# Six row buffers of four history positions in place of twenty, in a gather-and-score kernel

## The chip, the cores and the metric

The kernel runs on one core of one Trainium2 chip. The metric is the device time of the core in microseconds (us), the median of three runs. A core has five engines that run side by side and meet only at semaphores: PE (TensorE, matrix products and transposes), DVE (VectorE), ACT (ScalarE), POOL (GpSimd) and SP (SyncE, which only issues transfers). Here POOL does nothing but issue indirect transfers (gathers): each takes 128 row numbers, one for each partition, and fetches 128 rows of a table in device memory into an SBUF tile.

## What is computed

For each of 50001 items the reference makes two attention vectors from 32 neighbours. Then it scores, for each of 16384 users, the 100 items of a history against a target:

```python
a_sus = _neighbor_attn(E_in, near_full)
a_inf = _neighbor_attn(E_out, near_full)
...
h = jnp.concatenate([E_hist[history], hist_bi], axis=-1)
t = jnp.concatenate([E_tgt[target], tgt_bi], axis=-1)
x = h * t[:, None, :]
z = jax.nn.relu(jnp.einsum('bld,hd->blh', x, W1) + b1)
scores = jnp.einsum('blh,h->bl', z, W2[0])
exp_A = jnp.exp(scores)
mask = (history != target[:, None]) & (history != 0)
exp_A = exp_A * mask
denom = jnp.sum(exp_A, axis=-1) ** BETA
attn = exp_A / denom[:, None]
result = h * attn[..., None]
s = jnp.sum(result)
...
return jax.nn.sigmoid(pred)
```

`h` and `t` have 128 numbers each (64 of the item's own, 2 x 32 of attention). Only the sum of `result` over everything is used, so the kernel needs of each history row its 128 numbers (for the score) and their sum (for the result).

## The kernel before

**Stage 1** (lines 127 to 269) builds two tables in device memory. `table` has a row of 129 floats for each item: the sum, then the 128 numbers of `h`. `ttab` has the 128 numbers of `t`. It gathers 32 neighbours for each item (L160) and is done at about 17,507 us. The change touches nothing in it.

**Stage 2** (lines 271 to 457) goes through the users in 128 chunks of 128 users (one user for each partition), and in each chunk through the 100 positions in 25 groups of four (`LG = 4`, `NG = 25`). That makes 3200 groups, numbered `s`. One pass of the loop at L432 lists the work of several groups at once, and every engine does its own part in exactly this order (the order is written by hand):

- `gather(s)`, POOL: four indirect transfers (L342) fill the row buffer `rows[s % HB]`, tile name `h`, with 4 x 129 floats for each partition. From group `HB` on, the first of the four waits until the buffer's old content is done with: until the transposes of group `s - HB` have signalled (PE, `turned`, L352), and until the DVE copy of its row sums has run (`hsum`, L370). Each gather also waits for the one issued eight before it, whose counter it shares.
- `turn(s)`, PE: four transposes `hT<-ident,h` (L360) into one of three PSUM tiles (`RP = 3`). It waits for the landing of the group, and for `times_target(s - 3)` (`LH = 3`).
- `hidden(s - 3)`: the product with W1, `z_ps<-xT,w1T` (L389) on PE, then bias and relu on ACT, `z<-z_ps` (L393). The product waits for the ACT step three groups before.
- `scored(s - 6)`, PE: the product with W2, `bank<-z,pick` (L400), added up over the 25 groups of a chunk in one PSUM bank (`LS = 6`).
- `sums(s)` and `times_target(s)`, DVE: the copy `hsum<-h` (L370), then `xT<-hT,tT` (L379), the transposed rows times the target. `xT` waits for the signal of the transposes.

Once a chunk POOL gathers the next chunk's target rows (L309, tile `t`), in the pass of group 5; PE turns them in the pass of group 15. Also once a chunk the scores are turned back, exponentiated, masked and summed (L406 to L427).

**The end** (lines 463 to 481) makes one number from all users, then the 16384 answers.

"Shown late" or "signalled late" below means: the profile has an instruction's start on PE, and the engine that waits for its signal starts much later although nothing else is left to wait for. A group's signals can be followed by the start of its `xT` on DVE, because `xT` waits for nothing but the transposes' signal.

Of the kernel before, what the change touches and what calls it, by code (L numbers as in the profile page):

```python
# [44 lines left out]
NG = L // LG  # L45
W = 1 + D
M = 2
HB = 20
RP = 3
LH = 3  # L50
LS = 6
# [6 lines left out]
def kernel(  # L58
# [60 lines left out]
    u_h = ctx.enter_context(tc.tile_pool(name="u_h", bufs=1))  # L119
    rows = [u_h.tile([P, LG, W], F32, name=f"h{i}") for i in range(HB)]  # L120
    hists = {}
# [149 lines left out]
    with (  # L271
# [15 lines left out]
        def writes(one):  # L287
            writers[-1].append(one)
            if len(writers) > RP:
                for other in writers[len(writers) - 1 - RP]:  # L290
                    covered(one, other)
            return one
# [8 lines left out]
        def after(one, other):  # L301
            tc.add_manual_dep(one.ins, other.ins.name, SYNC, reason="waited for once for all that follows")

        def covered(one, other):
            tc.declare_no_dep(one.ins, other.ins, reason="a later wait or one engine's order covers it")
# [32 lines left out]
        def gather(s):  # L338
            c, g = divmod(s, NG)
            for q in range(LG):  # L340
                l = g * LG + q
                got = landed[s, q] = nc.gpsimd.indirect_dma_start(  # L342
                    out=rows[s % HB][:, q, :],
                    out_offset=None,
# [4 lines left out]
                )  # L349
                if s >= HB:  # L350
                    if q == 0:
                        after(got, turned[s - HB, LG - 1])  # L352
                    if q < LG - 1:
                        covered(got, turned.pop((s - HB, q)))

        def turn(s):
            at[s] = next_bank()
            for q in range(LG):
                turned[s, q] = writes(
                    nc.tensor.transpose(at[s][:, q, :], rows[s % HB][:, q, 1:W], ident)  # L360
                )
# [175 lines left out]
```

## Time and profile before

| | us |
|---|---|
| median of three runs (35853.54 to 35863.02) | 35858.32 |
| profiled execution, its time | 35866.87 |
| profiled execution, its span (first to last instruction) | 35865.1 |
| stage 1, to the last neighbour gather | about 17,507 |
| stage 2, first to last gather of history rows | 17507.9 to 35794.6 |
| from the last gather's start to the end of the span | 70.5 |

The profile's page gives each engine's busy time, the costliest groups of instructions with the idle time ahead of them on their engine, and what ended that idle time ("issue": nothing that the profile shows; "remote": a semaphore signal whose sender the profile cannot match). The timeline view has one row for each instruction: start, duration, engine, line, operation, tiles, and in square brackets the idle time before it. The windows view has the busy time and the count of instructions of each engine in a stretch, with the clock granted to PE (1.00 is full speed) and the transfers' rate. Durations on PE are modelled, starts are measured.

The busy shares over the whole span mix two stages that have different limits, so stage 2 has to be read by itself.

### The profile page before, as it was taken

What the parts mean: (1) busy time and instruction counts of PE and PEld (TensorE: products, weight loads), DVE (VectorE), ACT (ScalarE), POOL (GpSimd) and SP (SyncE); (2) the same over time, 40 slices, a digit from 0 to 9 for tenths busy, and PEclk for the clock granted to TensorE, in tenths of its full rate; (3) what the DMA queues carried; (4) which work ended last, traced back from release to release, by engine and by line L of the source; (5) the groups of instructions that cost most, each with busy time, mean ns of one, the idle gap of its engine ahead of it and who ended that gap; (6) DMA issues with size and microseconds to landing.
All of it is one profiled execution on the core that took longest, in us unless ns stands there. A gap on an engine that the chain in (4) does not pass through costs nothing. (4 is left out here: it accounts for less than half of the span.)

```text
span 35865.1 us, 102226 instructions
## 1 busy us (share of the span) xinstructions
PE 10007.5 (28%) x26243; PEld 3227.4 (9%) x26243; DVE 6894.8 (19%) x9965; ACT 2682.2 (7%) x5698; POOL 25707.9 (72%) x25446
## 2 busy tenths in 40 slices
PE   0000000000000000000255555555555555555555
PEld 0000000000000000000011111111111111111111
DVE  2222222222222222222111111111111111111111
ACT  0000000000000000000011111111111111111111
POOL 7777777777777777777766666666666666666666
PEclk9999999999999999999877777777777777777777
DMA  2111111111111111111111111111111111111111
GB/s 46 27 27 27 27 28 29 27 27 27 27 30 27 27 27 27 30 28 25 36 47 47 48 48 47 48 47 48 47 47 47 47 48 47 47 47 48 47 47 44
DMA packets 1027940, 1362.19 MB, mean 38 GB/s; under 512 B 559904, under 2 KB 614432, under 8 KB 1027360
## 3 DMA queue, kind: packets, MB, share of 16 engines
q0 software_dynamic: 814080, 1265.42, 14.7%
q10 hardware_dynamic: 100480, 38.63, 0.6%
q1 hardware_dynamic: 112800, 51.60, 0.6%
q8 instruction: 218, 3.57, 0.0%
q14 instruction: 362, 2.97, 0.0%
HBM read 1315.31 MB, written 51.50 MB: 38 GB/s over the span
## 5 line engine op out<-in xcount | busy, mean ns | idle before, releaser
L342 POOL DMA_INDIRECT h<-table,hidx x12800 | 12109.6, 946 | 6019.4 <-issue 3368.4
L160 POOL DMA_INDIRECT v<-in_egeo_dram,nidx x12512 | 13476.5, 1077 | 4012.6 <-issue 3944.0
L379 DVE TENSOR_TENSOR xT<-hT,tT 128x512 f32<-128x512 f32 x3200 | 2194.9, 690 | 15148.4 <-remote 9884.4
L321 PE MATMUL hT<-ident,t 128*128 128x128 f32 x128 | 46.8, 366 | 17630.5 <-DMA t<-ttab,tidx 17495.1
L389 PE MATMUL z_ps<-xT,w1T 128*128 128x512 f32 x6400 | 4194.4, 743 | 1745.1 <-ACT z L393 1355.8
L360 PE MATMUL hT<-ident,h 128*128 128x128 f32 x12800 | 2514.7, 328 | 5417.8 <-DVE xT L379 3698.5
L400 PE MATMUL bank<-z,pick 128*25 128x512 f32 x6400 | 4009.4, 714 | 0.0
L175 DVE TENSOR_TENSOR prod<-v,own_ps 128x4096 f32<-128x4096 f32 x196 | 864.4, 4410 | 12858.7 <-DMA v<-in_egeo_dram,nidx 12801.8
L393 ACT ACTIVATE z<-z_ps,b_sb 128x512 f32<-128x512 f32 x3200 | 2139.1, 687 | 15632.6 <-remote 8858.8
L360 PEld LDWEIGHTS hT<-ident,h 128*128 128x128 f32 x12800 | 1621.6, 163 | 8577.3 <-DVE xT L379 4769.4
L321 PEld LDWEIGHTS hT<-ident,t 128*128 128x128 f32 x128 | 19.2, 150 | 17772.6 <-issue 17573.6
L192 ACT ACTIVATE ex<-sc,top 128x32 f32<-128x32 f32 x782 | 227.8, 291 | 16704.6 <-DVE top L186 10993.0
L208 DVE TENSOR_TENSOR wv<-v,ex 128x1024 f32<-128x1024 f32 x782 | 1378.4, 1874 | 355.9 <-ACT ex L192 346.8
L389 PEld LDWEIGHTS z_ps<-xT,w1T 128*128 128x128 f32 x6400 | 1175.8, 230 | 1959.9 <-ACT z L393 1527.8
L182 DVE TENSOR_REDUCE sc<-prod 128x128 f32<-128x4096 f32 x196 | 864.5, 4411 | 6.7
L216 DVE TENSOR_REDUCE att<-wv 128x128 f32<-128x4096 f32 x196 | 864.1, 4409 | 6.0
L400 PEld LDWEIGHTS bank<-z,pick 128*25 128x25 f32 x6400 | 435.4, 109 | 3115.6 <-issue 3115.6
L370 DVE COPY hsum<-h 128x4 f32<-128x4 f32 x3200 | 567.8, 177 | 13.4 <-DMA h<-table,hidx 12.9
L415 PE MATMUL hT<-ident,flat 25*128 25x25 f32 x512 | 67.9, 255 | 1041.1 <-ACT flat L406 442.5
L309 POOL DMA_INDIRECT t<-ttab,tidx x128 | 121.1, 946 | 55.0 <-issue 54.4
L415 PEld LDWEIGHTS hT<-ident,flat 25*128 25x128 f32 x512 | 53.4, 176 | 1189.1 <-ACT flat L406 498.2
L192 ACT ACTIVATION_READ_ACCUMULATOR ex<-sc,top 128x1 f32 x782 | 146.1, 187 | 0.0
(53 smaller groups left out, 849.4 us busy)
## 6 DMA issues: line engine op xcount, KB each, us to landing
h<-table,hidx POOLq DMA_INDIRECT x12800
v<-in_egeo_dram,nidx POOLq DMA_INDIRECT x12512
table<-row ACTq DMA_DIRECT2D x22, 1096.5 KB
own<-in_egeo_dram SPq DMA_DIRECT2D x23, 544.0 KB
row<-in_ehist_dram SPq DMA_DIRECT2D x23, 544.0 KB
ttab<-in_etgt_dram ACTq DMA_DIRECT2D x1, 12500.0 KB
ttab<-row SPq DMA_DIRECT2D x22, 544.0 KB
hidx<-in_history_dram SPq DMA_DIRECT2D x32, 200.0 KB
```

The lines of the kernel that those rows point to most:

```text
L160: nc.gpsimd.indirect_dma_start(out=v[:, m, k].rearrange("p t d -> p (t d)"), out_offset=None, in_=egeo, in_offset=bass.IndirectOffsetOnAxi ...
L175: nc.vector.tensor_tensor(prod[:, 0:n].rearrange("p m k t d -> p m k (t d)"), v.rearrange("p m k t d -> p m k (t d)"), own_ps[:, 0:n].to_b ...
L182: nc.vector.tensor_reduce(sc[:, 0:n].rearrange("p m t k -> p m k t"), prod[:, 0:n], AX.X, ALU.add)
L208: nc.vector.tensor_tensor(wv[:, m, t].rearrange("p d k -> p k d"), subs[b]["v"][:, m, :, t, :], ex[:, m, t, :].rearrange("p (k o) -> p k o ...
L216: nc.vector.tensor_reduce(att[:, 0:n], wv[:, 0:n], AX.X, ALU.add)
L342: got = landed[s, q] = nc.gpsimd.indirect_dma_start(out=rows[s % HB][:, q, :], out_offset=None, in_=table, in_offset=bass.IndirectOffsetOn ...
L360: nc.tensor.transpose(at[s][:, q, :], rows[s % HB][:, q, 1:W], ident)
L370: copy = nc.vector.tensor_copy(users[c]["hsum"][:, g * LG : (g + 1) * LG], rows[s % HB][:, :, 0:1].rearrange("p q o -> p (q o)"),)
L379: times[s] = nc.vector.tensor_tensor(xT[s % XB], at.pop(s), users[c]["tT"].to_broadcast([D, LG, P]), ALU.mult)
L389: first[s] = nc.tensor.matmul(z_ps[s % RP], w1T, xT[s % XB], start=True, stop=True)
L393: second[s] = nc.scalar.activation(z[s % ZB], z_ps[s % RP], AF.Relu, bias=b1_sb)
L400: third[s] = nc.tensor.matmul(bank[c % 2], pick[:, g, :], z[s % ZB], start=g == 0, stop=g == NG - 1)
```

## The change

```diff
-HB = 20
+HB = 6
```

`HB` is the number of row buffers. It is used in `rows` (L120), in `gather` (L343, L350 to L354), and in `turn` and `sums`, which look up the buffer. A buffer holds 4 x 129 x 4 = 2064 bytes for each partition, so the pool shrinks from 41,280 to 12,384 bytes. The product of the scores runs on PE in both kernels (`scored`, L400, is the same in both); no instruction is added, removed or moved.

What differs is a wait. The rows are POOL's own list of instructions, around groups 5 and 6 of the first chunk; `h_102` is the sixth row buffer, `h_103` the seventh, `h_97` the first, and in square brackets stand the counters that an instruction waits for. Before:

```order
12540 L342 DMA h_102<-table,hidx 128x129 [waits DMASW1_49]
12541 L342 DMA h_103<-table,hidx 128x129 [waits DMASW2_49]
12542 L342 DMA h_103<-table,hidx 128x129 [waits DMASW3_49]
12543 L342 DMA h_103<-table,hidx 128x129 [waits DMASW4_49]
12544 L342 DMA h_103<-table,hidx 128x129 [waits DMASW5_49]
12545 L342 DMA h_104<-table,hidx 128x129 [waits DMASW6_49]
```

And now:

```order
12540 L342 DMA h_102<-table,hidx 128x129 [waits DMASW1_49]
12541 L342 DMA h_97<-table,hidx 128x129 [waits DMASW2_49,DVE_49,PE_49]
12542 L342 DMA h_97<-table,hidx 128x129 [waits DMASW3_49]
12543 L342 DMA h_97<-table,hidx 128x129 [waits DMASW4_49]
12544 L342 DMA h_97<-table,hidx 128x129 [waits DMASW5_49]
12545 L342 DMA h_98<-table,hidx 128x129 [waits DMASW6_49,DVE_49,PE_49]
```

Group 6 writes the first buffer again and so waits for DVE and PE. Before, the first group with such a wait was group 20. From group 20 on the lists have the same waits at the same places; the signal that is waited for is that of the group six before in place of twenty before.

## The prediction

> **What bounds the kernel now.** I read the page's groups first, because stage 1 and stage 2 share nothing but POOL:
>
> ```profile
> span 35865.1 us, 102226 instructions
> L342 POOL DMA_INDIRECT h<-table,hidx x12800 | 12109.6, 946 | 6019.4 <-issue 3368.4 <-remote 2070.2 <-DMA h<-table,hidx 265.3
> ```
>
> In stage 2 POOL is busy for 12.1 ms and idle for 6.0 ms. The 3368.4 us of "issue" over 10,991 times are 0.3 us between one gather and the next, part of its pace. The 2070.2 us of "remote" are something else, so I went to the windows and then to the timeline of one piece:
>
> ```profile
> 17507.00:35795.00 18288.00, 9953.97 (x26078) 3209.49 (x26078) 2675.07 (x7508) 2255.17 (x3686) 12229.91 (x12928) 0.72 0.19 47
> 17720.00:26000.00 8280.00, 4549.62 (x11852) 1467.41 (x11850) 1215.62 (x3409) 1026.75 (x1676) 5538.13 (x5856) 0.73 0.19 47
> 26000.00:35790.00 9790.00, 5330.40 (x14068) 1717.61 (x14068) 1442.01 (x4050) 1216.95 (x1990) 6547.72 (x6923) 0.72 0.19 47
> ```
>
> ```profile
> 26455.99 0.94 POOL L342 DMA_INDIRECT h<-table,hidx  x1 [5.54 <-remote]
> 26459.74 0.95 POOL L342 DMA_INDIRECT h<-table,hidx  x1 [0.31 <-issue]
> ...
> 26499.76 0.95 POOL L342 DMA_INDIRECT h<-table,hidx  x1 [0.30 <-issue]
> 26506.86 0.95 POOL L342 DMA_INDIRECT h<-table,hidx  x1 [6.16 <-remote]
> ```
>
> POOL runs in bursts. From 26455.99 to 26459.74 stand three steps of 1.25 us, so a group takes 5.0 us; to 26499.76 it issues 36 transfers (43.77 / 1.25 + 1), nine groups; then it stands 6.16 us. At 1.25 us the stage's 12,928 issues would take 16,160 us of the window's 18,288, so 2,128 us are such pauses. The pace with pauses is very even: 5856 issues in 8280 us and 6923 in 9790 us are both 1.414 us each, and this burst has 50.87 / 36 = 1.413.
>
> What POOL waits for is on DVE, whose `xT` starts when PE's transposes have signalled. Same piece:
>
> ```profile
> 26455.76 0.69 DVE L379 TENSOR_TENSOR xT<-hT,tT 128x512 f32<-128x512 f32 x1 [14.63 <-remote]
> ...
> 26457.77 0.68 DVE L379 TENSOR_TENSOR xT<-hT,tT 128x512 f32<-128x512 f32 x1
> ...
> 26463.90 0.69 DVE L379 TENSOR_TENSOR xT<-hT,tT 128x512 f32<-128x512 f32 x1 [1.65 <-PE hT L360]
> ...
> 26466.70 0.69 DVE L379 TENSOR_TENSOR xT<-hT,tT 128x512 f32<-128x512 f32 x1 [2.03 <-PE hT L360]
> ...
> 26475.81 0.69 DVE L379 TENSOR_TENSOR xT<-hT,tT 128x512 f32<-128x512 f32 x1 [8.34 <-issue]
> ...
> 26495.41 0.69 DVE L379 TENSOR_TENSOR xT<-hT,tT 128x512 f32<-128x512 f32 x1 [18.83 <-remote]
> ...
> 26506.63 0.69 DVE L379 TENSOR_TENSOR xT<-hT,tT 128x512 f32<-128x512 f32 x1 [10.42 <-remote]
> ```
>
> ```profile
> 26465.62 0.66 PE L360 MATMUL hT<-ident,h 128*128 128x128 f32 x4
> 26468.04 0.66 PE L360 MATMUL hT<-ident,h 128*128 128x128 f32 x4
> 26470.46 0.66 PE L360 MATMUL hT<-ident,h 128*128 128x128 f32 x4
> 26496.15 1.11 PE L360 MATMUL hT<-ident,h 128*128 128x128 f32 x4 [12.99 <-issue]
> 26502.44 2.08 PE L389 MATMUL z_ps<-xT,w1T 128*128 128x512 f32 x2 [5.18 <-ACT z L393]
> 26504.45 1.90 PE L400 MATMUL bank<-z,pick 128*25 128x512 f32 x2
> ```
>
> Call the first `xT` that of group n (those of n+1, n+2 and n+4 are left out). Groups n to n+3 come in 2 us (signals that were pending), n+5 and n+6 follow one another by 2.8 us, then n+7 comes after 9.1 us, n+8 after 19.6 us and n+9 after 11.2 us, when POOL has been still for a while. The transposes of n+6, n+7 and n+8 start on PE at 26465.62, 26468.04 and 26470.46; `xT` follows 1.1 us later for n+6 and 24.9 us later for n+8. So while transfers stream, PE's signals come later and later, and a pause of POOL lets them out at once. The profile doesn't say why. Whatever it is, it limits the average, since the pauses come out at the same share everywhere. The bound of stage 2 is this pair: streaming delays PE's signals, late signals fill the row buffers, and full buffers stop the streaming.
>
> **The change, part by part.** No instruction is added or removed, so PE, DVE and ACT have the same work; the score product is on PE before and after. One wait moves: group s on POOL waits for transposes s-6 in place of s-20. Behind it on POOL stand the rest of the gathers and, once a chunk, the target gather, which is issued ten groups (57 us) before PE turns it: no one waits for that. What the wait costs has three terms.
>
> (1) *The steady part.* After a pause, POOL starts group n+20 now, because transposes n have signalled, and may start n+20+j once n+j have. With six buffers it starts n+6 at the same signal and may start n+6+j under the same condition on n+j. At 0.23 + 5.0 j us after the signal its schedule is the same, the next pause comes at the same j (j = 9: due 45.2 us after the signal, transposes n+9 signal at 50.9), and it ends the same way. What can differ is that PE now waits for a landing. The landing is read at the start of the stage, where nothing is ahead:
>
> ```profile
> 17512.10 0.95 POOL L342 DMA_INDIRECT h<-table,hidx  x1 [0.30 <-issue]
> 17514.60 0.20 DVE L370 COPY hsum<-h 128x4 f32<-128x4 f32 x1 [3.63 <-DMA h<-table,hidx]
> ```
>
> 2.50 us from the fourth issue to the first reader. Groups n to n+5 have landed before the signal. Group n+6 is issued from 26455.99, its fourth transfer at 26459.74, and lands at 26462.2, before PE starts on it at 26465.6. n+7 lands at 26467.2, and its transposes start at 26468.04. n+8 lands at 26472.2, 1.8 us after PE started on it before (26470.46), but its signal reaches DVE only at 26495.4, so 1.8 us disappear in a delay of 24.9 us. Later groups have landed well before their signals too. I take 0 us for this term; the cover is the delay of PE's signals. If the cover fails, 1.8 us in each burst of 50.9 us (18,288 / 50.9 = 359 bursts) are 647 us. Below nothing the bound is the pauses altogether, -2,128 us.
>
> (2) *The start.* POOL ran its 20 buffers full while signals were already late:
>
> ```profile
> 17533.46 0.69 DVE L379 TENSOR_TENSOR xT<-hT,tT 128x512 f32<-128x512 f32 x1 [3.75 <-PE z_ps L389]
> 17566.36 0.69 DVE L379 TENSOR_TENSOR xT<-hT,tT 128x512 f32<-128x512 f32 x1 [15.79 <-remote]
> 17701.75 0.95 POOL L342 DMA_INDIRECT h<-table,hidx  x1 [4.46 <-remote]
> ```
>
> At 17701.75 POOL starts group 32: 131 issues since the window's start at 17507 (three of them target gathers) took 195 us, where the even pace gives 185. So the first long stall cost some 10 us. With six buffers POOL stops first before group 11, which waits for transposes 5 (17566.36), and the bursts begin there. I take half, -5 us; the ends are 0 and -12.
>
> (3) *The tail.* When POOL has issued the last transfer, PE still owes up to 20 groups:
>
> ```profile
> 35794.57 0.95 POOL L342 DMA_INDIRECT h<-table,hidx  x1 [0.31 <-issue]
> 35800.10 0.69 DVE L379 TENSOR_TENSOR xT<-hT,tT 128x512 f32<-128x512 f32 x1 [16.73 <-remote]
> 35843.64 0.69 DVE L379 TENSOR_TENSOR xT<-hT,tT 128x512 f32<-128x512 f32 x1 [1.65 <-PE hT L360]
> 35803.00:35843.00 40.00, 40.00 (x129) 13.28 (x127) 13.22 (x36) 11.07 (x17) 0.00 (x0) 0.96 0.00 1
> ```
>
> From 35800.10 the last 19 `xT` go at (35843.64 - 35800.10) / 18 = 2.42 us each, with PE at 0.96 of its clock. With six buffers 14 groups fewer are owed: -14 x 2.42 = -34 us. Against that, those 14 groups of PE work now lie inside the stream, where they may lengthen the pauses a little; I put 0 to +10 us on it and take 4. So -30.
>
> On the clock in that tail the Trainium skill has a rule against the change ("TensorE: Matmul & The Clock Gate", section "Part 1: The HAM clock gate"): PE falls to half clock after an idle window of about 3.4 us and needs as long a busy one to come back. The trace agrees for the slow stretches (the step from 26496.15 has 1.11, 2.08 and 1.90 us, against 0.66 us for the transposes at 26465.62). If all six last groups ran at that half clock, they would take 6 x 5.09 = 30.5 us in place of 14.5, and the gain of the tail would be about 14 us, not 30.
>
> Sum: 0 - 5 - 30 = -35 us on the profiled execution, 35,865 to 35,830 us of span. Its time (35,866.9) is 8.5 us over the median of the runs shown, 0.02%, and I carry the difference over to that median: 35,858 - 35 = **35,823 us**.
>
> **The rivals.**
>
> *A, the forecast:* same bursts, a shorter tail: 35,823 us; its own range is 35,740 to 35,900 (the pauses 4% shorter or longer, 85 us).
>
> *B, the signals come late later.* At the start, where PE took each group as it landed, `xT` of the fourth group (17533.46) is the first that is late, some 26 us after the window's start; in a burst PE, with 20 full buffers, has late signals after some 11 us (26466.70 is prompt, 26475.81 isn't). If PE paced by landings gains 14 us of prompt signals in each burst, a pause of 6.16 us comes once in 65 us and not in 50.9: 18,288 x (0.121 - 0.095) = 480 us less, 35,343 us. Against it: up to n+6 PE is not paced even with six buffers, and the pauses have kept one share in all stretches.
>
> *C, slower: PE's landing wait is not covered.* Place: the transposes of n+8 and after in PE's list, with the products of earlier groups (n+5, n+2) queued behind them. If a signal is late by a fixed time after its instruction has started, a late start is a late signal, transposes n+9 come 1.8 us later, and each pause grows by that: +647, 36,470 us. It decides from the point at which a landing (2.5 us after the fourth issue) comes after PE's start: n+7 has 0.8 us to spare. For it: PE's list has one order, and a blocked head blocks all. Against: signals pend for up to 25 us.
>
> *D, the pauses vanish.* If the delay came of the depth itself (20 groups pending), POOL would run through: 35,823 - 2,128 = 33,695 us. Against: the 20 buffers are never pending in PE, which has three `hT` tiles.
>
> *E, the change does nothing at all:* 35,858, if the tail's gain is lost in pauses; it lies in A's range.
>
> **How the numbers follow.** A with E 0.70, B 0.13, C 0.15, D 0.02. Prediction: A's, 35,823. Partial forms of B and C are likelier than their full prices, so the range takes in about half of each: 35,580 to 36,150. About 0.2% (72 us, 35,787 to 35,930) is what a measurement here can tell from no change. A lies 36 us above the lower of these and 107 under the upper; I give it 0.56 within, 0.12 below, 0.02 above. With B and D faster (0.14, 0.01 of which falls inside), and C slower (0.02 of which falls inside): faster 0.26, same 0.59, slower 0.15.
>
> **What would show it.** Right: the rows of POOL's gathers again 1.414 us apart on average, "remote" idle near 2,000 us, bursts of eight or nine groups, PE's count and clock in the windows as before, and 30 to 40 us between the last gather and the last `xT` gone. For B: longer bursts at the same pause. For C: transposes that wait for the landing of `h`, ahead of longer pauses. Wrong altogether if POOL's average pace leaves 1.41 us by more than 1%, for then the limit isn't what the bursts share but the depth of the buffers.

## The result, and the profile after

The changed kernel takes 35826.7 us (median, 35822.42 to 35836.81), the one before, timed beside it, 35861.34 us (35853.18 to 35867.87): 34.6 us less, ratio 0.9991 with a 95% interval of 0.9983 to 0.9999. The forecast was 35,823 us. The change lies inside the 0.2% that a measurement here can barely tell from none, though the slowest of the 14 runs with six buffers is still faster than the fastest of the 14 with twenty.

The span on the page of the changed kernel:

```profile
span 35824.9 us, 102240 instructions
```

The row of the history gathers in the view of the tile `h` (count; least, median and most ns of one; start of the first and of the last in us):

```profile
L342 POOL DMA_INDIRECT h<-table,hidx x12800: 938/944/1029, 17509.2 to 35798.5; - x197
```

The waits of POOL ahead of these gathers (us in all, times, longest):

```profile
POOL h L342 <- remote: 2045.9, 572, 10.7
POOL h L342 <- PE z_ps L389: 156.9, 155, 5.7
POOL h L342 <- PE hT L360: 115.9, 64, 7.4
```

The idle time named "remote" was 2070.2 us, and is 2045.9. The windows (busy us and counts of PE, weight loads, DVE, ACT and POOL; then PE's clock, transfer share, GB/s):

```profile
17720.00:26000.00 8280.00, 4635.47 (x11870) 1479.45 (x11870) 1216.18 (x3414) 1026.49 (x1678) 5525.64 (x5857) 0.74 0.19 47
26000.00:35750.00 9750.00, 5469.49 (x14004) 1748.76 (x14004) 1434.55 (x4033) 1212.55 (x1981) 6504.17 (x6894) 0.74 0.19 47
```

In the 8280 us up to 26000 POOL issues 5857 transfers, and before the change 5856: 1.414 us each, here and in the second window. The timeline of POOL shows bursts as before; these are the first gather of a burst, its last one, and the first of the next:

```profile
26403.79 0.94 POOL L342 DMA_INDIRECT h<-table,hidx  x1 [3.17 <-remote]
...
26447.48 0.94 POOL L342 DMA_INDIRECT h<-table,hidx  x1 [0.30 <-issue]
26454.74 0.94 POOL L342 DMA_INDIRECT h<-table,hidx  x1 [6.32 <-remote]
```

From 26403.79 to 26447.48 are 35 steps of 1.25 us, so 36 transfers, then a stop of 6.32 us: 50.95 us for 36, nearly to the digit the burst that the prediction quotes (50.87 us). That burst is a long one and not the average. Counted over POOL's timeline from 17720 to 35700, with a stop being an idle time over 0.6 us, there are 580 stops before and 598 after; 281 and 275 of the bursts between them have eight or nine groups, many of the rest have one, and the mean is 22 and 21 transfers.

What is new is on PE. In the waits of PE inside stage 2 (17720 to 35750) there is now a large row for the landing of the rows, which the kernel before does not have:

```profile
PE hT L360 <- DVE xT L379: 3100.4, 681, 16.4
PE hT L360 <- DMA h<-table,hidx: 1360.3, 720, 12.7
```

So PE does wait for landings, 1360.3 us over 720 times, and POOL's pace doesn't show it.

The time came out of the end. On POOL's timeline and then on DVE's, the last gather and the last three `xT`:

```profile
35798.51 0.94 POOL L342 DMA_INDIRECT h<-table,hidx  x1 [0.30 <-issue]
```

```profile
35794.86 0.69 DVE L379 TENSOR_TENSOR xT<-hT,tT 128x512 f32<-128x512 f32 x1 [1.64 <-issue]
35801.10 0.69 DVE L379 TENSOR_TENSOR xT<-hT,tT 128x512 f32<-128x512 f32 x1 [4.88 <-remote]
35801.89 0.69 DVE L379 TENSOR_TENSOR xT<-hT,tT 128x512 f32<-128x512 f32 x1
```

When the last gather starts, two groups are owed, where 19 were before, and the last `xT` comes 3.4 us later and not 49.1 us. The account of the two profiled executions, whose spans differ by 40.2 us:

| | before | after | difference |
|---|---|---|---|
| first history gather | 17507.9 | 17509.2 | +1.3 |
| first to last history gather | 18286.7 | 18289.3 | +2.6 |
| last gather's start to the end | 70.5 | 26.4 | -44.1 |

The start of stage 2, on POOL's timeline, has the stops that were expected there, but no gain:

```profile
17567.93 0.94 POOL L342 DMA_INDIRECT h<-table,hidx  x1 [2.42 <-remote]
17583.32 0.94 POOL L342 DMA_INDIRECT h<-table,hidx  x1 [10.70 <-remote]
17595.24 0.94 POOL L342 DMA_INDIRECT h<-table,hidx  x1 [7.24 <-remote]
17646.44 0.94 POOL L342 DMA_INDIRECT h<-table,hidx  x1 [6.57 <-PE hT L360]
17689.47 0.94 POOL L342 DMA_INDIRECT h<-table,hidx  x1 [2.14 <-remote]
17698.61 0.94 POOL L342 DMA_INDIRECT h<-table,hidx  x1 [4.46 <-PE z_ps L389]
```

Less the usual 0.30 each, these are 31.7 us of standing. Before, 131 issues in 195 us left 195 - 131 x 1.25 = 31 us. The stops came earlier and in smaller pieces, and their sum stayed.

### The profile page after: what moved, and what is told of

The parts are those of the page before. It is cut to its first block, busy times and chain, and to the rows that moved or that the text cites. A ratio compares the mean times of both kernels' runs of the same rounds, so it can differ in the third digit from the quotient of the medians.

```text
span 35824.9 us, 102240 instructions
## 1 busy us (share of the span) xinstructions
PE 10256.2 (29%) x26243; PEld 3278.1 (9%) x26243; DVE 6892.6 (19%) x9965; ACT 2682.2 (7%) x5698; POOL 25673.2 (72%) x25446
## 5 line engine op out<-in xcount | busy, mean ns | idle before, releaser
L342 POOL DMA_INDIRECT h<-table,hidx x12800 | 12076.6, 943 | 6055.5 <-issue 3379.8
L160 POOL DMA_INDIRECT v<-in_egeo_dram,nidx x12512 | 13475.2, 1077 | 4015.2 <-issue 3949.6
L389 PE MATMUL z_ps<-xT,w1T 128*128 128x512 f32 x6400 | 4320.4, 764 | 1330.3 <-ACT z L393 1021.5
L400 PE MATMUL bank<-z,pick 128*25 128x512 f32 x6400 | 4105.5, 730 | 0.0
L400 PEld LDWEIGHTS bank<-z,pick 128*25 128x25 f32 x6400 | 442.5, 111 | 3241.0 <-issue 3241.0
```

The costliest lines, as they stand in the source:

```text
L160: nc.gpsimd.indirect_dma_start(out=v[:, m, k].rearrange("p t d -> p (t d)"), out_offset=None, in_=egeo, in_offset=bass.IndirectOffsetOnAxi ...
L342: got = landed[s, q] = nc.gpsimd.indirect_dma_start(out=rows[s % HB][:, q, :], out_offset=None, in_=table, in_offset=bass.IndirectOffsetOn ...
L389: first[s] = nc.tensor.matmul(z_ps[s % RP], w1T, xT[s % XB], start=True, stop=True)
L400: third[s] = nc.tensor.matmul(bank[c % 2], pick[:, g, :], z[s % ZB], start=g == 0, stop=g == NG - 1)
```

## The experiments

Two questions were left: is the gain the tail and nothing else, and what sets the pace of 1.414 us a gather: the depth of the buffers, PE's work, or the transfers themselves? "Owed" is the number of groups whose `xT` starts after the last gather has. The three sets below ran on three chips, the first on one where even the kernel before takes 31809.79 us, so each kernel is compared only with the kernel before of its own set.

### Three and two buffers, more work on POOL, less on PE, on a chip without pauses

```diff
-HB = 6
+HB = 3
```

> Three row buffers in place of six, nothing else. Theory 'shared limit' (streaming and the signals of PE share something that allows one gather per 1.414 us on average; the buffers only have to cover a group's way to PE, and their number sets how much PE owes at the end): the pace stays at 1.41 us, pauses come oftener and are shorter, 35,815 to 35,860 us. Rival 'uncovered landing' (each wait of PE for a landing is a later signal): with three buffers the group n+3 lands 6.5 us after the signal that frees POOL where PE wants it at 2.0 us, so at least 4.5 us in each of 359 bursts, 37,400 us or more.

Measured: 31808.16 us against 31809.79, ratio 0.9999 (0.999 to 1.0009). On the page of this kernel:

```profile
L342 POOL DMA_INDIRECT h<-table,hidx x12800 | 12086.8, 944 | 3899.9 <-issue 3842.3
L160 POOL DMA_INDIRECT v<-in_egeo_dram,nidx x12512 | 11813.6, 944 | 3821.4 <-issue 3771.1
```

"Remote" is no longer among the causes: of 3899.9 us idle, 3842.3 are the 0.3 us between gathers. PE's signals are in time here (over all 3200 groups `xT` starts at most 0.9 us after the last transpose of its group has started), three buffers never stop POOL, and a history gather costs (12086.8 + 3899.9) / 12800 = 1.249 us. That is the burst's own pace on the chip with pauses. Stage 1 differs too: its row on the page of the kernel before, on the other chip, is

```profile
L160 POOL DMA_INDIRECT v<-in_egeo_dram,nidx x12512 | 13476.5, 1077 | 4012.6 <-issue 3944.0
```

(13476.5 + 4012.6) / 12512 = 1.398 us a gather there, 1.250 here. So nearly the whole difference between the chips is one of the gathers' pace, in both stages. Depth could not be judged here, since nothing ever waits for it.

```diff
-HB = 6
+HB = 2
```

> Two row buffers in place of six, nothing else. Shared limit: a group's way is 3.75 us of issue, 2.5 us to the landing and about 1.2 us of transposes, 7.5 us against 10 us for two groups of issue, so with prompt signals POOL isn't stopped; 35,800 to 36,200 us. Uncovered landing: n+2 lands 6.5 us after the signal and PE wants it at 1.4 us, over 5 us in each burst and bursts that are three times as many, 40,000 us or more.

Measured: 31810.82 us, ratio 1.0 (0.9991 to 1.001). With gathers in time, even two buffers do.

```diff
+    fill = u_h.tile([P, 352], F32, name="fill")
...
     def gather(s):
...
+            nc.gpsimd.memset(fill, 0.0)
```

> Six buffers, and one memset of a tile of its own (128x352) on POOL ahead of each group's gathers, about 0.45 us by the 128x128 one of 0.2 us in the profile. Shared limit: POOL's pauses (0.66 us a group on average) shrink by what the memset takes and the time stays, 35,800 to 35,880 us. Rival 'pauses on top of POOL's own pace': 3200 x 0.45 us are added, 37,270 us.

Measured: 32683.82 us, ratio 1.0274 (1.0257 to 1.0291), 874 us more. On its page:

```profile
L341 POOL MEMSET fill<- 128x352 f32 x3200 | 1313.2, 410 | 1.1
L344 POOL DMA_INDIRECT h<-table,hidx x12800 | 12113.0, 946 | 3452.3 <-issue 3418.5
```

1313.2 us of memsets came in and the gathers' idle time, against that with three buffers above, shrank by 3899.9 - 3452.3 = 448 us, which leaves 866 us. My expectation rested on pauses that could swallow this work. There are none on this chip, so POOL's own list is the bound and the expectation missed.

The last kernel of this set leaves the product with W2 out for 23 of the 25 groups of each chunk:

```diff
+            if g not in (0, NG - 1):
+                return
...
```

> Six buffers; the product with W2 is left out for 23 of the 25 groups of each chunk (first and last stay), which takes 4 of 16 instructions a group from PE. If the shared limit is in the transfers alone: the pace stays at 1.41 us, 35,790 to 35,850 us. If PE's own instructions take their share of it: pauses shrink by a part of their 0.66 us a group, by 0.18 us if the share goes by a fit of the bursts' lengths to their counts, 35,250 us. If PE itself were the limit with its slow steps: a quarter of the work, pauses nearly gone, 33,900 us.

Measured: 31805.93 us, ratio 0.9999 (0.9989 to 1.0009). Where POOL's list is the bound, PE's work costs nothing.

### Six again, one buffer, half the gathers, a little work on POOL, on a chip with pauses

The change itself, once more:

```diff
-HB = 20
+HB = 6
```

> The change as it is, once more. Theory 'pauses' (the buffers' depth shows only in what PE owes at the end, and PE owes much only where its signals come late and POOL pauses): on a chip where the kernel before takes some 31,810 us POOL never pauses, PE is one group behind with either depth, and the ratio is 1.0000 within 0.0005; on one where it takes some 35,860 us the ratio is 0.9990. Rival 'depth has a gain of its own' (smaller buffers, other addresses): 0.999 on both.

Measured: 35902.88 us against 35934.28 of the kernel before, 31.4 us less, ratio 0.9991 (0.9982 to 1.0). Its groups, its windows, the waits of PE and the end of DVE's timeline:

```profile
L342 POOL DMA_INDIRECT h<-table,hidx x12800 | 12077.5, 944 | 6127.1 <-issue 3667.7 <-remote 1990.8 <-PE hT L360 178.2
```

```profile
17720.00:26000.00 8280.00, 4553.69 (x11850) 1462.44 (x11850) 1204.11 (x3412) 1020.46 (x1677) 5501.25 (x5831) 0.74 0.22 47
```

```profile
PE hT L360 <- DMA h<-table,hidx: 1443.5, 713, 12.1
```

```profile
35875.29 0.69 DVE L379 TENSOR_TENSOR xT<-hT,tT 128x512 f32<-128x512 f32 x1 [19.46 <-remote]
...
35886.82 0.69 DVE L379 TENSOR_TENSOR xT<-hT,tT 128x512 f32<-128x512 f32 x1 [1.66 <-PE hT L360]
```

8280 / 5831 = 1.420 us a gather, and a gain of the same size on another chip. Since two and three buffers gained nothing on the chip without pauses, the gain hangs on the pauses. The last gather starts at 35872.4; six groups are owed then, and the last `xT` comes 14.4 us later.

```diff
-HB = 6
+HB = 1
```

> One row buffer. Here nothing covers a group's way any more: 3.75 us to the fourth issue, 2.5 us to the landing, about 1.2 us of transposes, 7.5 us a group in place of 5.0. Theory 'a buffer has to cover the way, more is of no use': 15,650 + 3200 x 7.5 + 30 = 39,700 us on a chip without pauses, 41,500 us or more on one with them. Rival 'depth never decides': 31,810 or 35,830 us.

Measured: 42397.94 us, ratio 1.1799 (1.1777 to 1.182). The page:

```profile
L342 POOL DMA_INDIRECT h<-table,hidx x12800 | 12105.2, 946 | 12596.2 <-PE hT L360 9456.4
```

With one buffer each group is issued, landed and turned before the next: the 24,859 us of gathers (17510.4 to 42369.3) are 7.77 us a group, near the 7.5 that the way through one buffer was expected to take. The chain is in series and the wait has a name now (9456.4 us for the transposes, by their signal). PE's signals are all in time when gathers go at 1.94 us each: `xT` again starts at most 0.9 us after its last transpose has started.

The next one leaves two of the four gathers of each group out (zeros, written once at the start, stand in their place, so the output is not the reference's), while PE, DVE and ACT do everything as before in every group:

```diff
+    for one in rows:
+        nc.vector.memset(one, 0.0)
...
-            for q in range(LG):
+            for q in range(2):
...
```

> Six buffers; two of the four gathers of each group are left out, and the other two positions hold zeros; PE, DVE and ACT do the same work. Where there are no pauses: POOL needs 2 x 1.25 = 2.5 us a group against 2.42 us of PE, stage 2 is 8,160 us, 23,840 us in all; if PE's cold clock or its waits decide, up to 25,300 us (2.95 us a group). Where there are pauses: if the limit is one gather per 1.414 us, 17,507 + 9,230 + 30 = 26,770 us; if it is in PE's signals by themselves, 30,000 us and more.

Measured: 27008.25 us, ratio 0.7516 (0.7502 to 0.753). Its windows:

```profile
17520.00:26000.00 8480.00, 7421.74 (x23474) 2516.53 (x23475) 2367.28 (x6753) 2010.89 (x3319) 5530.03 (x5846) 0.94 0.22 47
```

PE now does twice as much for each gather (23474 instructions in 8480 us, against 11850 in 8280), at 0.94 of its clock, and the pace is 8480 / 5846 = 1.451 us a gather, 2% more than the 1.420 of the full kernel. Over the burst's own 1.25 us that is 0.20 us of standing for each gather, where the full kernel has 0.17. If the limit had come with PE's signals, twice as many of them for each gather would have doubled it to 0.34. It goes with the gathers. What the remaining 2% are stays open: a group takes 2 x 1.451 = 2.9 us here, not far above the 2.42 us that PE takes by itself at full clock.

```diff
+    fill = u_h.tile([P, 128], F32, name="fill")
...
     def gather(s):
...
+            nc.gpsimd.memset(fill, 0.0)
```

> Six buffers, and a memset of 128x128 on POOL ahead of each group's gathers, half the one before (0.2 us). Where there are no pauses POOL's list is the bound and 0.07 us (what was left of 0.41 us less the 0.14 us of idle time that it took up) to 0.2 us a group are added: 32,030 to 32,460 us. Where there are pauses they shrink by as much, and the time stays at 35,790 to 35,870 us.

Measured: 35912.77 us, ratio 0.9994 (0.9985 to 1.0003), 10 us above six buffers. The page:

```profile
L344 POOL DMA_INDIRECT h<-table,hidx x12800 | 12133.3, 948 | 5367.4 <-issue 3397.2
L341 POOL MEMSET fill<- 128x128 f32 x3200 | 716.9, 224 | 8.0 <-remote 3.1
```

716.9 us of work was added to POOL, and the gathers' idle time fell from 6127.1 to 5367.4 us, by 759.7. The pauses made room for nearly all of it, so what stands fast is the average pace of the gathers.

### Thirteen and three buffers, less on PE, and POOL filled past the pace, on a chip with pauses

The kernel before takes 35938.8 us here (35930.76 to 35948.62).

```diff
-HB = 6
+HB = 13
```

> Thirteen row buffers in place of twenty, a point between the two kernels. If the gain is the tail (what PE still owes when the last gather is issued), it should lie between: on a chip with pauses (before 35,860 to 35,930 us) about 10 to 12 groups owed at the last gather in place of some 19, so 7 to 9 x 2.42 = 17 to 22 us less than before, ratio 0.9994 to 0.9995, with gathers again 1.41 to 1.42 us apart. If the gain came from a waiting that starts below some depth, thirteen would read as twenty (0 us, still 15 to 19 owed). On a chip without pauses (before about 31,810 us) only one group is ever owed, and the time is the same within 0.1%.

Measured: 35921.57 us, 17.2 us less than before, ratio 0.9996 (0.9987 to 1.0005). DVE's timeline at the end; the last gather starts at 35880.43:

```profile
35884.50 0.69 DVE L379 TENSOR_TENSOR xT<-hT,tT 128x512 f32<-128x512 f32 x1 [9.12 <-remote]
...
35886.51 0.69 DVE L379 TENSOR_TENSOR xT<-hT,tT 128x512 f32<-128x512 f32 x1
35890.98 0.69 DVE L379 TENSOR_TENSOR xT<-hT,tT 128x512 f32<-128x512 f32 x1 [3.71 <-PE hT L360]
35893.53 0.69 DVE L379 TENSOR_TENSOR xT<-hT,tT 128x512 f32<-128x512 f32 x1 [1.78 <-PE hT L360]
...
35903.21 0.69 DVE L379 TENSOR_TENSOR xT<-hT,tT 128x512 f32<-128x512 f32 x1 [1.65 <-PE hT L360]
```

Ten groups are owed here, and the last `xT` comes 22.8 us after the last gather; with six buffers above it was six groups and 14.4 us. The pace is that of six buffers: 5829 gathers in the window where six had 5831. With thirteen, PE waits for landings 25.1 us in all, and the pace is the same with and without these waits. The 17.2 us sit at the lower end of the 17 to 22 expected, and the gap to before isn't resolved by the interval alone. The rows show ten owed groups at this depth, between those of six and of twenty; each depth but six has one trace.

```diff
-HB = 6
+HB = 3
```

> Three row buffers in place of twenty, where the landing wait of TensorE has the least cover. Theory (the limit is shared by transfers and signals, and a landing wait disappears in the signals' delay): on a chip with pauses ratio 0.998 to 1.000, 30 to 45 us less than before, gathers 1.41 to 1.42 us apart in short bursts of three to five groups. Rival (the landing wait is uncovered once the depth is small): each burst costs 1.8 us or more, and with bursts of four groups (some 20 us) that is 900 bursts, +1,600 us, ratio 1.045. On a chip without pauses: the same as before within 0.1%, as measured there already.

Measured: 35946.33 us, ratio 1.0002 (0.9993 to 1.0012), 7.5 us above before where I expected 30 to 45 below. Page, waits of PE, and DVE's last `xT`:

```profile
L342 POOL DMA_INDIRECT h<-table,hidx x12800 | 12107.0, 946 | 6143.9 <-issue 3611.2
```

```profile
PE hT L360 <- DMA h<-table,hidx: 6531.4, 2897, 8.4
```

```profile
35919.86 0.69 DVE L379 TENSOR_TENSOR xT<-hT,tT 128x512 f32<-128x512 f32 x1 [4.90 <-remote]
35921.36 0.69 DVE L379 TENSOR_TENSOR xT<-hT,tT 128x512 f32<-128x512 f32 x1 [0.73 <-remote]
35922.03 0.68 DVE L379 TENSOR_TENSOR xT<-hT,tT 128x512 f32<-128x512 f32 x1
```

The tail is short: three groups after the last gather (35918.2), 3.9 us. But the stage is longer. PE waits 6531.4 us for landings, in nine groups of ten, 4.5 times as long as with six buffers on the chip before (1443.5 us). The rival price of 1,600 us did not come. On the same chip thirteen buffers, which have next to no such waits, take 18365.8 us from the first to the last gather; three take 18408.5 us, 42.7 us more. POOL's gathers took 30 us more of that (12107.0 against 12076.7 us) and its idle time 12 us (6143.9 against 6131.8), but this split explains nothing: between the two kernels of the change the gathers became 33 us shorter (12109.6 to 12076.6 us) and the idle time 36 us longer, in a stage of the same length. So neither theory had the size. The landing wait is covered even here but for some 43 us at most, and what the 43 us are stays open.

The product with W2 again left out for 23 of 25 groups:

```diff
+            if g not in (0, NG - 1):
+                return
...
```

> Six row buffers, and the product with W2 is left out for 23 of the 25 groups of each chunk, so the output is not the reference's. On TensorE that takes away some 2 of 12 instructions a group. If the limit of the stage belongs to the transfers alone, the pace stays 1.41 to 1.42 us a gather and the time that of six buffers (ratio about 0.999). If TensorE's own instructions have a share in it (each of its instructions costs signal time), the pauses shrink with them: two twelfths of 2,000 to 2,100 us are 350 us, ratio 0.989; if the pauses come of the length of TensorE's list alone, more, -580 us. On a chip without pauses: 1.000.

Measured: 35835.93 us, ratio 0.9972 (0.996 to 0.9983). That is 102.9 us under before and some 71 us more of a gain than six buffers alone had in their set. The thirteen buffers of this set say the same: from the first to the last gather it is 18296.9 us here and 18365.8 there, 69 us less. Window:

```profile
17720.00:26000.00 8280.00, 3562.27 (x9204) 1573.63 (x9204) 1238.96 (x3421) 1037.63 (x1682) 5530.43 (x5847) 0.63 0.22 47
```

PE has 22% fewer instructions (9204 against 11850 with six buffers in the set before), and POOL goes 0.3% faster (5847 against 5831). The expectation had counted two instructions of twelve; by the 22% of the windows its price would be some 450 us and not 350. Neither theory had it: PE's work has a share in the pace, but some 70 us of some 2,000.

Last, a larger memset ahead of each group, so that POOL by itself is slower than the pace with pauses:

```diff
+    fill = u_h.tile([P, 1024], F32, name="fill")
...
     def gather(s):
...
+            nc.gpsimd.memset(fill, 0.0)
```

> Six row buffers, and POOL gets a memset of 128x1024 floats (an estimate of 1.0 us by the 224 ns and 410 ns of the smaller ones, 1.15 if it goes with size) ahead of each group. That makes its own list 5.0 + 1.0 to 1.15 - 0.14 = 5.9 to 6.0 us a group, more than the 5.66 to 5.69 of the pace with pauses. If pauses and POOL's work share one limit (an average rate of transfers that must not be passed), the pauses all but vanish, TensorE's signals become prompt, 'remote' idle falls from 2,000 us to under 300, and the stage takes 3200 x 5.9 to 6.0 = 18.9 to 19.2 ms, so 36,400 to 36,800 us in all. If a pause is a cost of its own per so many transfers, it is added on top: 18.9 to 19.2 ms + 2.0 ms, 38,400 to 38,800. On a chip without pauses: 3200 x 5.9 to 6.0 after 15,650 us of stage 1, 34,550 to 34,900.

Measured: 36390.2 us, ratio 1.0126 (1.0108 to 1.0145). Page, waits and DVE's timeline near the end:

```profile
L341 POOL MEMSET fill<- 128x1024 f32 x3200 | 3110.5, 972 | 1.5
```

```profile
POOL h L344 <- issue: 3411.5, 12539, 0.3
POOL h L344 <- remote: 8.1, 2, 4.2
```

```profile
35849.62 0.69 DVE L381 TENSOR_TENSOR xT<-hT,tT 128x512 f32<-128x512 f32 x1 [0.36 <-PE hT L362]
35855.89 0.69 DVE L381 TENSOR_TENSOR xT<-hT,tT 128x512 f32<-128x512 f32 x1 [1.06 <-PE hT L362]
35861.75 0.69 DVE L381 TENSOR_TENSOR xT<-hT,tT 128x512 f32<-128x512 f32 x1 [0.81 <-PE hT L362]
```

This is 451.4 us above the kernel before of its set, and six buffers alone were 31.4 under theirs, so 3110.5 us of added work cost some 483. "Remote" fell from 1990.8 to 8.1 us, `xT` runs every 5.9 us, and in 99 groups of 100 it starts within 0.6 us of the start of its last transpose. The stage has 18,852 us (17510.7 to 36362.6), 12,928 issues at 1.458 us each. So at 1.458 us on average next to nothing is late, and where POOL's own list would go faster than 1.420, pauses fill the difference. They are no cost of their own: they are what is left between POOL's own pace and a limit on the average.

Of the depths tried where there are pauses, six shows the largest gain (0.9991 on two chips; thirteen 0.9996, three 1.0002), but these intervals overlap; one buffer costs 18%. Where there are no pauses, two, three and twenty are the same.

## Why the prediction came out right

**The bound.** That a pair of streaming and late signals keeps an even pace is what happened: 5857 against 5856 gathers in the same window, and nearly as many long bursts (275 against 281). What lies under the pair, which the prediction left open, is a limit on the average pace of gathers on such a chip, 1.41 to 1.42 us: shown by the memsets (717 us of them cost 10 us, 3110.5 us cost some 483) and by half the gathers with the same PE work (1.451 us). PE's work has a small share in it (some 70 us of some 2,000, where 22% of its instructions were gone). Stage 1, with 1.398 us a gather against 1.250 on the other chip, suggests the same limit there; that it is the same was only argued.

Two readings of the working were off without harm to the forecast. The signals pend longer than its 25 us. In its own burst the transposes of group n+9 start at

```profile
26472.88 0.66 PE L360 MATMUL hT<-ident,h 128*128 128x128 f32 x4
```

and their `xT` is the one at 26506.63, 33.8 us later; the longest of that trace, in the long first stall, is 66 us. And its 359 bursts of 50.9 us are too few: 580 stops were counted, so the price of 1.8 us in each burst would have been some 1,040 us and not 647.

**Steady part, 0 us.** Measured +2.6 us from the first to the last gather, start included. PE's new wait for landings was there (1360.3 us, C's mechanism) and was covered, as the working had it. Three buffers bear this out: 6531.4 us of such waits, and a stage at most 43 us longer than with thirteen buffers, which have next to none. That it is the delay of the signals which covers the wait is argued from the burst; the runs show that the wait does not reach POOL's pace.

**Start, -5 us.** The place was right: POOL's first stop is at 17567.93, ahead of group 11. The gain was wrong. I took the 10 us by which the first 195 us lie over the even pace for a price of the long first stall, half of which smaller stops could save. Group 32 starts 193.8 us after the first history gather before and 194.4 us after it now: the standing stayed, as it stays anywhere in the stage. The forecast gave the depth of the buffers a share here that it denied it in the steady part.

**Tail, -34 and +4 us.** Mechanism right, size off: -44.1 us in the profile. I counted 14 groups fewer (20 less 6), but six buffers need not be full when the last gather goes out. Two were owed in this run, six in the second one, four with the small memset; before it was 19. 17 groups at 2.42 us are 41 us, and the rest is the uneven end (3.4 us to the last `xT`, then 23.0 us and not 21.5). With thirteen buffers ten were owed. So the term depends on where in a burst the last gather falls, by some 10 us: last gather to end is 26.4 us in this run and 35.9 in the second one.

The Trainium skill ("TensorE: Matmul & The Clock Gate", section "Part 1: The HAM clock gate") has PE at half clock after an idle window. The traces show this in the tail too. In the second run with six buffers PE stood 11.8 us, and its granted clock is 0.50 from 35872 to 35884, most of the 14.4 us; in thirteen buffers one step, from 35886.51 to 35890.98, takes 4.5 us, and then four steps from 35893.53 to 35903.21 take 2.42 each. But the price that the prediction put on it, 30.5 us for six groups, did not come. Three of the six groups had been transposed before the last gather and only their signals were pending, and no tail stays at half clock to its end.

**The rivals.** B: the bursts are not longer (a mean of 21 transfers, 22 before). C: its wait came, its price of 647 us did not. D: the pauses stayed, 2045.9 us; only POOL's own work removes them. E was wrong by the tail.

In the profiled executions the sum is -40.2 us and not -35: the start gave nothing where 5 us were put, the pauses took 2.6 us where 4 were put, and the tail gave 10 us more. So the errors went in part against one another. That the medians, with -34.6 us, meet the -35 so closely is partly luck: the tail alone differs by 10 us between the two traced executions with six buffers.

## What to carry to other kernels

When an engine's stops come out at the same share everywhere, ask first whether they are the cost or only what fills the time up to a limit: add work to the engine that stands, and if the stops shrink by as much, a deeper or shallower buffer will change the ends of the stage more than its pace, as long as it still covers the way of one group (here one buffer did not: 42,398 us). The ends are then worth counting by themselves: here depth beyond what covers a landing added only work owed after the last transfer. A new wait in the profile, here one of 1,360 us, need not show in the time where something else already holds the engine's results up.

## What the hardware showed beyond expectation

The same kernel takes 31,810 us on one chip and 35,860 to 35,940 us on others. Nearly all of it lies in the indirect gathers: 1.249 us each in both stages on the one (read with three buffers); on the others 1.398 us in stage 1, where the gather itself is longer (1071 to 1077 ns in place of 944), and 1.41 to 1.42 us in stage 2, where it has its 944 ns but POOL stands still in between.

The three-buffer kernel ran on both kinds of chip. The queue of the gathers on its two pages (packets, MB, share of the span of 16 engines), first without and then with pauses:

```profile
q0 software_dynamic: 814080, 1265.42, 19.9%
q0 software_dynamic: 814080, 1265.42, 17.6%
```

19.9% of 31824 us and 17.6% of 35943 us are both some 6,330 us: the same packets take the same time. So the packets are not slower where there are pauses, and their engines are far from full.

With the pauses go signals of PE that reach DVE up to 34 us after their transposes have started, in the burst quoted, while gathers stream at 1.25 us, and that come out together when POOL stops; at 1.458 us on average next to none is late. Ends on PE are modelled, so the profile cannot tell whether the transposes end late or only their signal does. What in the chip holds them back, and why the chips differ, no run here tells.
